# Image 2's routed layer issued in half steps, norms spread a tile earlier: a two-layer attention kernel on one core

## The chip, the core and the metric

The kernel runs on one core of one Trainium2 chip. The metric is the time of one launch on the device in microseconds: 1705.04 us, the median of three runs (1703.87 to 1706.76). The core's engines are called PE or TensorE (matrix products and transposes), DVE or VectorE, ACT or ScalarE, POOL or GpSimd, and SP, which here only issues transfers.

## The reference

The input holds four images of 32 x 128 x 128 floats. Layer 0 turns each image into 128 channels (each 2 x 2 block of pixels gives four) by 64 x 64 places, and lets the channels' rows attend to each other by cosine; here is the core of it:

```python
energy = jnp.einsum('bci,bcj->bij', q, q)
d = jnp.sqrt(jnp.diagonal(energy, axis1=1, axis2=2))
attn = jax.nn.softmax(energy / (d[:, :, None] * d[:, None, :]), axis=-1)
out = gamma * jnp.einsum('bcj,bij->bci', q, attn) + xs
...
t = t + _L1_attn_ref(_ln_t(t), Wk, Wq, Wv)
t = t + _L1_ffn_ref(_ln_t(t), router_w, router_b, expert_w, expert_b)
```

In the kernel's terms: 4096 rows of 128 values per image (after the reshapes), all pairs of rows scored, exponentials, products, a division by the sums. Layer 1 takes the result as tokens of 128 values: a linear attention, which comes down to one 128 x 128 Gram matrix of the normalised tokens per image, a small chain of products of that matrix with the weights, and one product per token; then a router picks two of eight experts for each token and the two expert products are added with their weights.

## The kernel before

**Score tiles.** Each image's 4096 rows are cut into 8 chunks of 512, handled in four pairs kc. `attend` walks over the pairs of chunks jc <= i, four tiles of 128 x 512 for each: 144 tiles per image, 152 for the last image, whose end is ordered differently. A tile is a product `pe` (L607), an exponential on ScalarE with its sum (L610), and a product `po` (L495). Scores are symmetric, so the transposed half is not computed again: VectorE turns 32 x 32 blocks (L419), SP sends them to DRAM and back (L528, L543) to swap them, and some five tiles later TensorE multiplies the turned block (`pg`, L431) while ScalarE sums it (L436).

**The program is an order written by hand.** Everything is a Python generator, and the order of issue on TensorE, VectorE, ScalarE and SP is the order in which the generators are advanced. The loop at the end of the kernel advances `attend` by half a tile: one half ends just before `pe`, the other after the tile's other products. Each other stream that is due is advanced once in each half. So two yields are one tile step of a stream; `idle(n)` is n such steps. GpSimd's operations are pinned to the same order where it matters.

**Streams beside the tiles.** They are of two kinds:

- `timed`: for each image b the preparation of the next one, `prep(b + 1, kc)` for the four pairs of chunks. An entry (steps, begin, end, count) is advanced evenly, count times between begin and end, in per cent of the image. `prep` loads the pixels (L308), turns them into qT, sums squares (L295, L296), takes the power -1/2 on GpSimd (L164), spreads these norms over columns into `wide` (L388, VectorE), transposes `wide` on TensorE into the bank `pnorm` (L397), and multiplies the pixels with it (`scale_all`, L372) to give qn.
- `steady`: layer 1 of an image. It starts at 84% of its own image and runs on through most of the next, one step about every tile. `close_rows(kc)` ends layer 0 for a pair of chunks: transposed sums `pbd`, division (L759), the residual, statistics of each token on VectorE, their power on GpSimd (L164, `rsa`, then `nba` at L688), the normalised rows `xn` on ScalarE (L694), and TensorE's Gram products `pgram` (L726). Then come `matrix` and `attention_rows`, and after them `sorted_experts(h)` for each half h of the tokens.

**Sorted experts.** A half has 2048 tokens with two experts each. VectorE computes where each token goes in a list sorted by expert. GpSimd scatters the rows to DRAM, 32 indirect transfers of 128 rows (L1049). Then the list is read back in 20 pairs of 128-row tiles. For the pair g at position `at` of the loop: SP loads it (L1077) at g, TensorE transposes it (L1118) three positions later, ScalarE copies the transposes out (L1087), TensorE multiplies them with the expert's weights (L1111) at the fourth, VectorE applies the token's weight (L1093) and SP stores the result in `ys` (L1097). A position has two yields: `load` and the evictions of the position before fall into one half of a step, the products into the other.

**Gathers.** After that, GpSimd gathers each token's two results from `ys` and adds them to the token's row in `acc` by indirect transfers that accumulate (L1162): 8 for each group of four tiles, 64 for both halves. `fetch` (on ScalarE's queue, L1147) fills `acc` before, `put` (SP, L1153) writes a finished group to the output. The first half is gathered when the second half's scatters are issued. For images 0 and 1 a gather is issued per step; for image 2 two per step, with a free step after every four (`rate == 2`). Image 3 has no image after it, so it does not sort: `last_parts` multiplies all experts.

**The end.** For image 3 only `close_rows` is a stream (`first_parts`). When the tiles are through, what is left of `steady` is issued, image 2's layer first, then image 3's, and then `last_parts`. The names to follow in the code are `prep`, `close_rows` (`close_stats`, `normalise`, `gram_rows`), `sorted_experts` with `load`, `products`, `fetch`, `put`, and the tuples in the loop at the end.

Of the kernel before, what the change touches and what calls it, by code (L numbers as in the profile page):

```python
# [22 lines left out]
def kernel(  # L23
# [45 lines left out]
    B, C, H, W = x.shape  # L69
# [108 lines left out]
    def idle(n):  # L178
        for _ in range(2 * n):
            yield  # L180
# [167 lines left out]
    def prep(b, kc, st):  # L348

        ahead = 2 if b == 0 and kc == 1 else 5
        xa = load_quarters(b, kc)
        if b == 0:
            load_tokens(st["T"][:, ts(kc, 8), :], b, 8 * kc, 8)
            xx = rows_of_image(b, kc, st)
        for _ in range(ahead):
            yield
        qT = chunks_of(b, kc, st)
        for s in range(2):  # L360
            turn_quarters(s, xa, qT)
            yield
        if b > 0:
            xx = xin.tile([P, 8, HW2, 2], F32, tag="xx", name=f"xx_{b}_{kc}")
            load_tokens(xx.rearrange("p k w r -> p k (w r)"), b, 8 * kc, 8)
        ss = stat.tile([P, 2 * NJ], F32, tag="ss", name=f"ss_{b}_{kc}")

        def scale(s, spread, view):
            qn = channels(b, kc, s, st)
            own = slice(s * 64, s * 64 + 64)  # L370
            for r2 in range(2):
                nc.vector.tensor_tensor(  # L372
                    qn[ts(r2, 64)].rearrange("p (j a t) -> p a j t", a=4, t=S),
                    xx[own].rearrange("p (a k) (h t) r -> p r a (k h) t", a=4, h=2)[:, r2],
                    view(spread[own]),
                    ALU.mult,
                )
        rn = stat.tile([P, 2 * NJ, 1], F32, tag="rn", name=f"rn_{b}_{kc}")
        for s in range(2):
            squares(b, kc, s, qT, ss)  # L380
            if s == 1:
                pow_neg_half(rn[:, :, 0], ss)
            yield
        for _ in range(ahead - 2):
            yield
        wide = work.tile([P, NJ, 2, 64], F32, tag="qs", name=f"wide_{b}_{kc}", bufs=2)
        for s in range(2):
            nc.vector.tensor_copy(wide[:, :, s], rn[:, ts(s, NJ)].to_broadcast([P, NJ, 64]))  # L388
        yield

        def scale_all(bank):
            for s in range(2):
                scale(s, bank, lambda ap: ap.rearrange("p (j a t) -> p a j t", a=4, t=S))

        bank, done = hold(f"pnorm_{b}_{kc}", scale_all)
        for j in range(NJ):
            nc.tensor.transpose(bank[:, ts(j, P)], wide[:, j].rearrange("p s c -> p (s c)"), ident)  # L397
        yield
        done()
        yield  # L400
# [251 lines left out]
    def layer1(b, st):  # L652
# [76 lines left out]
        def close_rows(kc):  # L729


            def missing():
                return len(st["o"]) < 2 * kc + 2 or any(
                    st["got"][c] < NCH - c - (alone and c == NCH - 1) for c in (2 * kc, 2 * kc + 1)
                )

            late_rows = alone and kc >= 2
            last_rows = alone and kc == 3

            while "exps" not in st if last_rows else missing():  # L740
                yield from idle(1)
            while b > 0 and kc == 0 and not states[b - 1].get("sorted"):
                yield from idle(1)
            den, rd = (stat.tile([P, 2 * NJ], F32, tag=nm, name=f"{nm}_{b}_{kc}") for nm in ("den", "rd"))
            nc.vector.tensor_reduce(den, st["sums"][:, ts(kc, 2 * NJ), :], AX.X, ALU.add)
            nc.vector.reciprocal(rd, den)
            wide = work.tile([P, NJ, 2, 64], F32, tag="grp", name=f"rdx_{b}_{kc}", bufs=2)
            for s in range(2):
                one = rd[:, ts(s, NJ)][:, :, None]
                nc.vector.tensor_scalar(wide[:, :, s], one.to_broadcast([P, NJ, 64]), gam, None, ALU.mult)  # L750
            df = work.tile([P, 8, HW2, 2], F32, tag="df", name=f"df_{b}_{kc}", bufs=1)

            def divide(pb):
                for s in range(2):
                    own = slice(s * 64, s * 64 + 64)
                    o = st["o"][2 * kc + s]
                    for r2 in range(2):
                        rows = slice(r2 * 64, r2 * 64 + 64)
                        nc.vector.tensor_tensor(  # L759
                            df[own].rearrange("p (a k) (h t) r -> p r a (k h) t", a=4, h=2)[:, r2],  # L760
                            o[rows].rearrange("p (a j t) -> p a j t", a=4, t=S),
                            pb[own].rearrange("p (j a t) -> p a j t", a=4, t=S),
                            ALU.mult,
                        )

            yield
            if not last_rows:
                yield
                yield
            pb, done = hold(f"pbd_{b}_{kc}", divide)  # L770
            for j in range(NJ):
                nc.tensor.transpose(pb[:, ts(j, P)], wide[:, j].rearrange("p s c -> p (s c)"), ident)
            yield
            while missing():
                yield from idle(1)
            done()
            if not late_rows:
                yield
                yield
            tk = T[:, ts(kc, 8), :]  # L780
            nc.vector.tensor_tensor(tk, tk, df.rearrange("p k w r -> p k (w r)"), ALU.add)
            bs, stats = batch_stats("a", 8 * kc, 8)
            for j in range(8):
                stats[j]()
                if j == 3:
                    yield
                    yield
            close_stats("a", 8 * kc, 8, bs)
            yield from idle(1 if late_rows else 2)
            k = 8 * kc  # L790
            normalise(range(k, k + 4), rsa, nba)
            if late_rows:
                for j in range(k + 4, k + 8):
                    nc.vector.tensor_scalar(
                        xn[:, j, :D], T[:, j, :], rsa[:, j, :], nba[:, j, :], ALU.mult, ALU.add
                    )
            yield
            if last_rows:
                keep_running(36)
                done = gram_rows([k + j // 2 + 4 * (j % 2) for j in range(8)])  # L800
                yield
                done()
                return
            done = gram_rows(range(k, k + 4))
            yield
            done()
            if not late_rows:
                normalise(range(k + 4, k + 8), rsa, nba)
            yield
            done = gram_rows(range(k + 4, k + 8))  # L810
            yield
            done()
            if alone and kc < 3:
                for g in (2 * kc, 2 * kc + 1):
                    yield
                    done = transpose_rows(g)
                    yield
                    done()
# [151 lines left out]
        def sorted_experts(h):  # L970
# [72 lines left out]
            for n in range(2 * HR):  # L1043
# [19 lines left out]
                if n % 4 == 3 and (b < B - 2 or n % 8 == 7):  # L1063
                    yield from idle(1)
            turns[h].append("moved")
            xs_made[h][:], xs_read[h][:] = scatters, []
            yield from idle(3)

# [56 lines left out]
            for at in range(len(pairs) + 5):  # L1125
                if at < len(pairs):
                    load(*pairs[at])
                if done:
                    done()
                yield  # L1130
                turned, applied = (pairs[at - d] if 0 <= at - d < len(pairs) else None for d in (3, 4))
                done = products(turned, applied) if turned or applied else None
                yield
# [22 lines left out]
            rate = 1 if b < B - 2 else 2  # L1156
            fetch(groups[0])
            yield from idle(2)
            for g in groups:
                for n in range(8):  # L1160
# [5 lines left out]
                    if (n + 1) % rate == 0:  # L1166
                        yield
                        yield
                    if rate == 2 and n % 4 == 3:
                        yield from idle(1)  # L1170
                    if n == 3 and g != groups[0]:
                        put(g - 1)
                    if n == 3 and g != groups[-1]:
# [197 lines left out]
    timed = [(first, 0, 1, 2), (second, 0.5, 5.5, 10)]  # L1371
    for b in range(B):
# [5 lines left out]
            timed.append((setup_sorting(), 58, 98, 17))  # L1378
        if b + 1 < B:
            nxt = states[b + 1]  # L1380
            timed.append((prep(b + 1, 0, nxt), 52, 78, 16))
            timed.append((prep(b + 1, 1, nxt), 80, 99, 16))
        if b > 0:
            timed.append((input_rows(b, states[b]), 36, 47, 9))
        done = [0] * len(timed)
# [21 lines left out]
                pass  # L1407
        timed = []
        if b + 1 < B:
            timed.append((prep(b + 1, 2, nxt), 1, 22, 16))  # L1410
            timed.append((prep(b + 1, 3, nxt), 28, 52, 16))
    for steps, _ in steady:
        for _ in steps:
            pass
# [40 lines left out]
```

## Time and profile before

| | |
|---|---|
| median of three runs | 1705.04 us |
| the profiled execution | 1704.18 us |
| its span, first to last instruction | 1702.4 us |
| mean granted TensorE clock | 0.987 |
| score tiles of image 0, 1, 2, 3 begin at | 12.9, 355.9, 749.5, 1148.1 us |
| last exponential of image 3 | 1562.0 us |
| scatters of image 2 | 1299.3 to 1409.1 us |
| gathers of image 2 | 1449.8 to 1603.0 us |

The busiest engines and the costliest groups of the page:

```profile
PE 1629.5 (96%) x5288; PEld 858.7 (50%) x5288; DVE 910.2 (53%) x2343; ACT 913.3 (54%) x2863; POOL 630.5 (37%) x565
...
L1162 POOL DMA_INDIRECT acc<-ys,place x192 | 301.4, 1570 | 300.1 <-ACT pr L610 171.2
...
L726 PE MATMUL pgram<-xn 128*128 128x128 f32 x256 | 38.7, 294 | 34.7 <-ACT xn L694 34.4
```

A group's line gives the source line, engine, operation and tiles, then the busy time in all and the mean of one in ns, then the idle time of the engine just before these instructions and what ended most of it. "xn L694" stands for the instruction on ScalarE whose end released the waiting one. The time of the launch is some 2 us more than the span, which begins with the first instruction and ends with the last.

### The profile page before, as it was taken

To read this page: it belongs to the slowest core of one execution; us is meant where nothing else is said; L and a number is where in the kernel's file an instruction comes from. 1 tells how busy PE (TensorE), PEld (TensorE's weight loads), DVE (VectorE), ACT (ScalarE), POOL (GpSimd) and SP (SyncE) were. 2 spreads that over 40 slices of the span, in tenths; PEclk is the share of its full clock that TensorE was granted. 3 is DMA by queue.
4 is the path that set the end of the run, shared out by engine and by line. 5 is a ranking of instruction groups with operands and counts; after the bars stand their busy time and mean duration, and the time that the engine had idled before them with its cause. 6 is when DMAs were issued, how large, how long until landed. Compare 5 with 4: busy or idle time off the path is not lost.

```text
span 1702.4 us, 21468 instructions
## 1 busy us (share of the span) xinstructions
PE 1629.5 (96%) x5288; PEld 858.7 (50%) x5288; DVE 910.2 (53%) x2343; ACT 913.3 (54%) x2863; POOL 630.5 (37%) x565
## 2 busy tenths in 40 slices
PE   8999999999999999999999999999998999999288
PEld 5444444455544455555554455555554455546243
DVE  5443353666684443567486343557479333346187
ACT  3555445465655555556574555546565455555076
POOL 1000000001034532455454541454555540567666
PEclk9999999999999999999999999999999999999699
DMA  5554765654457777975688777895777867983201
GB/s 159 180 203 145 216 207 198 236 187 156 158 180 254 234 241 220 253 223 163 191 237 243 242 223 226 248 257 155 198 213 223 264 220 224 249 239 59 44 12 39
DMA packets 249067, 332.81 MB, mean 195 GB/s; under 512 B 31984, under 2 KB 176496, under 8 KB 234608
## 3 DMA queue, kind: packets, MB, share of 16 engines
q1 hardware_dynamic: 207312, 291.92, 53.5%
q0 software_dynamic: 33792, 25.58, 8.5%
q10 hardware_dynamic: 7840, 13.93, 2.7%
q8 instruction: 45, 0.74, 0.2%
q14 instruction: 78, 0.64, 0.1%
HBM read 160.78 MB, written 175.80 MB: 198 GB/s over the span
## 4 chain that ended last, share of the span: by engine, by line
PE 77%; DVE 10%; DMA 4%; POOL 3%; ACT 2%; issue 2%; SPq 1%; DVEq 0%; ACTq 0%; POOLq 0%
PE po L495 22%; PE pe L607 21%; PE pg L431 19%; PE pys L1111 3%; PE py L1247 2%; POOL acc L1162 2%; PE pgram L726 2%; PE pg L451 2%; DVE F L419 2%; PE pys L1118 1%; PE pat L852 1%; DVE df L759 1%; DMA blocks<-F 1%; SPq L543 1%; DMA F<-blocks 1%
## 5 line engine op out<-in xcount | busy, mean ns | idle before, releaser
L610 ACT ACTIVATE pr<-pe 128x512 f32<-128x512 f32 (+1 forms) x576 | 322.4, 560 | 533.1 <-PE pe L607 427.7
L495 PE MATMUL po<-pr,qT 128*128 128x512 f32 (+3 forms) x1152 | 551.2, 560 | 3.5 <-ACT o L500 2.2
L607 PE MATMUL pe<-qn,qn 128*128 128x512 f32 x896 | 459.1, 594 | 5.2 <-ACT pr L610 5.0
L431 PE MATMUL pg<-F,qT 128*128 128x512 f32 x880 | 450.3, 593 | 1.6 <-DMA F<-blocks 1.6
L1162 POOL DMA_INDIRECT acc<-ys,place x192 | 301.4, 1570 | 300.1 <-ACT pr L610 171.2
L419 DVE STREAM_TRANSPOSE F<-pr 128x512 f32<-128x512 f32 x440 | 307.4, 703 | 157.1 <-ACT pr L610 124.4
L495 PEld LDWEIGHTS po<-pr,qT 128*128 128x128 f32 x1152 | 215.0, 190 | 250.4 <-issue 223.6
L436 ACT ACTIVATE junk<-F 128x512 bf16<-128x512 f32 x440 | 272.7, 620 | 1.7 <-DMA F<-blocks 1.7
L431 PEld LDWEIGHTS pg<-F,qT 128*128 128x128 f32 x880 | 167.2, 191 | 197.0 <-issue 179.8
L1049 POOL DMA_INDIRECT xs<-xn,place x192 | 185.0, 963 | 165.5 <-ACT pr L610 99.8
L607 PEld LDWEIGHTS pe<-qn,qn 128*128 128x128 f32 x896 | 154.3, 190 | 116.2 <-issue 103.0
L440 DVE TENSOR_TENSOR o<-o,pg 128x512 f32<-128x512 f32 x110 | 75.2, 684 | 207.6 <-PE pg L431 185.7
L164 POOL TENSOR_TENSOR rn<-ss,neg_half 128x8 f32<-128x8 f32 (+1 forms) x17 | 27.7, 1629 | 388.7 <-DVE ss L296 388.7
L1093 DVE TENSOR_TENSOR results<-pys,xn 128x256 f32<-128x256 f32 x120 | 49.8, 415 | 183.8 <-ACT xn L1087 146.3
L610 ACT ACTIVATION_READ_ACCUMULATOR pr<-pe 128x1 f32 x576 | 111.8, 194 | 0.0
L1087 ACT ACTIVATE xn<-pys 128x256 f32<-128x256 f32 x120 | 45.3, 378 | 114.1 <-PE pys L1118 98.1
L1111 PEld LDWEIGHTS pys<-ew_sb,xn 128*128 128x128 f32 x468 | 70.2, 191 | 50.4 <-issue 48.8
L607 PE MATMUL pe<-qn 128*128 128x512 f32 (+3 forms) x256 | 91.0, 438 | 0.7 <-ACT qn L342 0.7
L436 ACT ACTIVATION_READ_ACCUMULATOR junk<-F 128x1 f32 x440 | 84.2, 191 | 0.0
L694 ACT ACTIVATE xn<-T,nba,rsa 128x128 f32<-128x128 f32 x120 | 49.2, 483 | 44.6 <-POOL nba L688 44.6
L726 PE MATMUL pgram<-xn 128*128 128x128 f32 x256 | 38.7, 294 | 34.7 <-ACT xn L694 34.4
L1111 PE MATMUL pys<-ew_sb,xn 128*128 x468 | 71.6, 274 | 0.0
(214 smaller groups left out, 1459.8 us busy)
## 6 DMA issues: line engine op xcount, KB each, us to landing
blocks<-F SPq DMA_DIRECT2D x110, 1024.0 KB
F<-blocks SPq DMA_DIRECT2D x220, 192.0 KB
F<-blocks SPq DMA_DIRECT2D x220, 128.0 KB
xn<-xs SPq DMA_DIRECT2D x114, 132.0 KB
ys<-results SPq DMA_DIRECT2D x114, 128.0 KB
F<-blocks SPq DMA_DIRECT2D x220, 64.0 KB
below<-F SPq DMA_DIRECT2D x31, 384.0 KB
T<-in_x_dram SPq DMA_DIRECT2D x64, 128.0 KB
```

The costliest lines, as they stand in the source:

```text
L419: f()
L431: nc.tensor.matmul(pg.rearrange("p (a f) -> p a f", a=4), st["qT"][i][:, ib, :], G[:, :, ib], start=(ib == 0), stop=(ib == NJ - 1),)
L436: nc.scalar.activation(junk, G[:, :, ib], AF.Copy, accum_out=st["sums"][:, NJ * i + ib, jc : jc + 1])
L440: nc.vector.tensor_tensor(st["o"][jc], st["o"][jc], pg, ALU.add)
L495: nc.tensor.matmul(row["po"][:, lo:hi], qT[blk // NJ][:, blk % NJ, :], w, start=start, stop=(row["left"] == 0))
L607: nc.tensor.matmul(pe[:, c0:], qn[jc][:, ts(j, P)], qn[i][:, c0:], start=True, stop=True)
L610: nc.scalar.activation(pr[:, c0:], pe[:, c0:], AF.Exp, accum_out=sums[:, t, i : i + 1]).ins
L726: nc.tensor.matmul(p[:, :D], xn[:, k, :D], xn[:, k, :D], start=(k == rows[0]), stop=(k == rows[-1]))
L1049: inst = nc.gpsimd.indirect_dma_start(xs[h], offset(place[:, i, k : k + 1]), xn[:, k, :], None)
L1093: nc.vector.tensor_tensor(result[:, :n], p[:, 2 * P : 2 * P + n * D].rearrange("p (j c) -> p j c", c=D), bufs[g % 6][:, :n, D : D + 1].to_ ...
L1111: nc.tensor.matmul(p[:, 2 * P + j * D : 2 * P + j * D + D], bufs[6 + g % 2][:, j, :D], weights[:, bass.ds(begins[2 * (g % 2) + j], D)], st ...
L1162: inst = nc.gpsimd.indirect_dma_start(accs[g][:, n % 4, :], None, ys, offset(place[:, i, k : k + 1]), compute_op=ALU.add)
```

## The change

Six edits, all in the order of issue; no operation is added or removed and nothing of the arithmetic differs.

1. `prep`: for images after the first, one more yield between the spreading of the norms (`wide`) and the transposes that read it.
2. `close_rows`: three idle steps instead of two between the statistics and the first normalised rows (all but the last two pairs of chunks of image 3, which keep one).
3. `sorted_experts`, image 2 alone (`hurried`): the yield between the evictions and the products of a position goes, so that a position takes half a step.
4. The free step after every four gathers of image 2 goes.
5. The counts of `prep` for images 1 to 3 are 17 instead of 16.
6. The third pair of chunks is prepared between 0.5% and 16% of the image instead of between 1% and 22%.

```diff
@@ prep
         for s in range(2):
             nc.vector.tensor_copy(wide[:, :, s], rn[:, ts(s, NJ)].to_broadcast([P, NJ, 64]))
         yield
+        if b:
+            yield
@@ close_rows
             close_stats("a", 8 * kc, 8, bs)
-            yield from idle(1 if late_rows else 2)
+            yield from idle(1 if late_rows else 3)
@@ sorted_experts
             turns[h].append("moved")
+            hurried = b == B - 2
...
                 if done:
                     done()
-                yield
+                if not hurried:
+                    yield
                 turned, applied = (pairs[at - d] if 0 <= at - d < len(pairs) else None for d in (3, 4))
                 done = products(turned, applied) if turned or applied else None
                 yield
...
                     if (n + 1) % rate == 0:
                         yield
                         yield
-                    if rate == 2 and n % 4 == 3:
-                        yield from idle(1)
@@ the loop at the end
-            timed.append((prep(b + 1, 0, nxt), 52, 78, 16))
-            timed.append((prep(b + 1, 1, nxt), 80, 99, 16))
+            timed.append((prep(b + 1, 0, nxt), 52, 78, 17))
+            timed.append((prep(b + 1, 1, nxt), 80, 99, 17))
...
-            timed.append((prep(b + 1, 2, nxt), 1, 22, 16))
-            timed.append((prep(b + 1, 3, nxt), 28, 52, 16))
+            timed.append((prep(b + 1, 2, nxt), 0.5, 16, 17))
+            timed.append((prep(b + 1, 3, nxt), 28, 52, 17))
```

## The prediction

> **What bounds the kernel now.** I read the page's 40 slices first, then the busy times by stretch, then who waited for whom around the hole, then GpSimd's timeline there.
>
> ```profile
> PE   8999999999999999999999999999998999999288
> POOL 1000000001034532455454541454555540567666
> PEclk9999999999999999999999999999999999999699
> ```
>
> TensorE is full nearly everywhere: what is added to its queue costs its own length, and what another engine does is free. The exception is slice 38, where it is 20% busy and its clock falls.
>
> ```profile
> 1449.00:1562.00 113.00, 113.00 (x385) 60.66 (x384) 50.34 (x120) 61.13 (x191) 71.92 (x48) 1.00 0.75 194
> 1562.00:1605.00 43.00, 12.98 (x94) 10.65 (x92) 10.54 (x38) 6.17 (x15) 36.44 (x25) 0.71 0.36 58
> ```
>
> The columns are TensorE, its weight loads, VectorE, ScalarE, GpSimd, then clock, DMA share and GB/s. While image 3 attends, TensorE has no hole at all; from 1562 to 1605 only GpSimd works (36.4 of 43 us).
>
> ```profile
> ACT xn L694 <- POOL nba L688: 34.1, 2, 33.3
> PE pgram L726 <- ACT xn L694: 29.6, 1, 29.6
> ```
>
> TensorE waits 29.6 us for ScalarE's normalised rows, and ScalarE 33.3 us for a scale from GpSimd.
>
> ```profile
> 1599.62 1.54 POOL L1162 DMA_INDIRECT acc<-ys,place  x1 [0.31 <-issue]
> 1601.46 1.54 POOL L1162 DMA_INDIRECT acc<-ys,place  x1 [0.30 <-issue]
> 1602.45 2.27 POOL L164 TENSOR_TENSOR rsa<-dm_a,neg_half 128x8 f32<-128x8 f32 x1
> ```
>
> That scale (the last pair of chunks of image 3) stands in GpSimd's queue behind the last gathers of image 2, one every 1.84 us (1.54 and 0.30 of issue). VectorE had finished its input at 1575.1 (the last sv_a of its timeline); the rows began at 1605.0. So the last layer of image 2 is late, not image 3.
>
> Two smaller holes come back with each image:
>
> ```profile
> PE pnorm L397 <- DVE F L419: 5.8, 3, 2.0
> ```
>
> and two waits of 2.1 us at L726 on ScalarE (tile 14 of images 2 and 3, in the timeline). After two of the three pnorm waits the clock is at half for 3.4 us (508.6 and 907.9).
>
> **What the Trainium skill says.** "DMA: Bandwidth & Descriptors", section "SWDGE vs HWDGE vs iDMA": a transfer that accumulates can be issued by GpSimd alone, whose cores compute the descriptors. The trace agrees: GpSimd is busy 1.54 us per gather of 128 rows, whether DMA is busy (1464) or quiet (1590). So the gathers have a floor of 64 x 1.84 = 118 us. "Trainium Architecture — The Big Picture", section "Inside one NeuronCore": each engine has its own instruction stream and meets the others through semaphores. So a small operation behind a gather waits for the gather, as at 1602. "TensorE: Matmul & The Clock Gate", section "What's actually happening": an idle window of about 3.4 us halves the clock until a busy one. Here the clock was at 0.5 from 1580.3 to 1611.1, and 16 Gram matmuls took 3.79 us where 8 took 0.89.
>
> **The change part by part.** A "tile" is one of the 144 score tiles of an image (152 in image 3), about 2.58 us of TensorE. I counted tiles at which each piece is issued in both programs, and took the tiles' times from the trace before.
>
> 1. *Half steps.* Image 2's pairs of sorted tiles (20 in each half) are issued twice per tile step instead of once. The first half's loop ends at tile 93, not 105; the second's at 116, not 128. The work is moved, not changed: a pair costs 0.66 us of TensorE (steps with a pair take 3.24, without 2.58). But in the old loop the transposes of a pair, the copy L1087 on ScalarE and the product that reads it were a whole step apart. Now every second product follows directly upon the transposes of the pair before it: nothing stands between the end of one step and the start of the next. TensorE then waits for ScalarE. From the timeline at 1398: TensorE is free at 1398.54, the copy starts 0.20 later, takes 0.38, then a handover of about 0.1 and a weight load of 0.11 to 0.19: 0.8 us. The programs show 16 such joints, 8 in each half: 13 us added. This wait is not in the trace; bounds are 0.5 (16 x 0.5 = 8) and 1.5 (24), should loads be late too. It can't gain. The loads L1077 are issued in SP's order behind stores that wait for VectorE; they land in 1.5 to 4.5 us by the DMA packets, and some 4 half steps (8 us) lie between, so I take no wait for them.
>
> 2. *Gathers.* With the first half's products done earlier, and without the free steps, the first gather moves from tile 109 to 102, the last four from the end of the program to tiles 137 and 138. Tile 102 began at 1426.8; 4 more pairs (2.6) and 8 joints (6.4) lie before it: 1436, against 1449.8 before. But 8 gathers need 14.7 us, and 4 tiles without pairs only 10.3. GpSimd keeps pace until group 4 (tile 122, now about 1503: 1486.5, 6 pairs, 13 us of joints), then lags. The 64 gathers end near 1565, while VectorE's input for the last scale comes at 1575 plus all delays. So the hole closes: 1605.0 less 1577.7 (1575.1, the power 1.7, the bias, handovers) is 27.4 us, and 2.7 us more as the clock stays up (16 Gram matmuls 3.79 to 1.78, six at L837 0.7). Gain 30.
>
> 3. *What is late next.* The first scale of image 3 (chunks 0 and 1) is issued at tile 136, behind 60 gathers. From 1504: groups 4 to 6 and four of group 7 are 28 x 1.84 = 51.5, so the power starts at 1555.6 and rows can start 2.2 later (1529.38 to 1531.56 before): 1557.8. ScalarE reaches them after the score of tile 139, a tile later than before because of idle(3): 1533.1 + 1.2 + 13 = 1547. It stands 10.7 us, with all the exponentials of later tiles behind it in its queue. TensorE needs the rows 1.4 us later than they used to be ready (1534.61 against 1533.2), so it stands 9.3 us, and about 2 more at half clock. Bounds: 0, if GpSimd keeps pace, and 17, if gathers take 2.1 us each. SP's stores of finished groups (L1153) also wait for gathers: that of group 5, about 1535, stands before the loads of the last turned block; these land near 1544 and are used at 1553. Hidden, with 9 us to spare.
>
> 4. *Norms, idle(3), third pair of chunks.* The copies to `wide` move ahead of the transposes by a tile, in all three images, and the third pair's to tile 9 from 14. The pnorm waits (5.8) go, with two half-speed windows (2 x 1.7). The Gram waits at tile 14 (2 x 2.1) go, as VectorE's squares for the next image no longer stand before the statistics, and the rows are asked for later. Sum 13.5. Against it, rows of four groups now fall on tiles 4 to 7 in a row, where ScalarE has 0.75 + 0.81 + 1.64 = 3.2 us per tile against TensorE's 3.0, and everything of the last layer is issued a tile later. I take 10 (bounds 4 and 14).
>
> Sum: -30 + 13 + 9.3 + 2 - 10 = -15.7. The profiled execution took 1704.18 us (its span is 1702.4): 1688.5. The median of the runs is 0.86 above it: 1689.
>
> **The rivals.**
>
> *A, GpSimd keeps pace.* If gathers find enough room, the scale at tile 136 isn't waited for: 11 us less, 1678. For it: part 3 rests on a count of 28 gathers without a gap. Against it: bursts in the trace never go below 1.84.
>
> *B, the half steps starve TensorE: slower.* The place is L1111/L1118 of image 2, tiles 81 to 116. If the loads or SP's order make each of the 40 pairs wait, not only the joints, the loss grows. For it: SP stood up to 8 us at L543 with loads behind. Against it: DMA share is 0.70 there, and the step gets longer as pairs get denser. At 2 us for each of 16 joints (32 us, 19 more than forecast) the time is 1708. It decides from 1.8 us per joint.
>
> *C, the hole stays in part.* If the gathers lag further (2.3 us each in the crowded stretch) the last scale is again behind them and the first wait doubles: part 3 costs 25 and the time is about 1702, no change.
>
> *D, joints cheap and small holes wholly gone:* 8 instead of 13, 13.5 instead of 10: 1680, within the forecast's own range.
>
> **How the numbers follow.** Forecast (with D) 0.60, A 0.17, B 0.15, C 0.08. The likeliest case's own range is 1680 to 1698. To leave out no more than two in ten the range takes in A to 1674 and the near part of B and C: 1673 to 1706. Two runs of this kernel tell about 0.2% apart (3.4 us). Faster: forecast and A, 0.77, and a little of C: 0.79. Same: most of C: 0.06. Slower: B: 0.15.
>
> **What would show it.** The hole after 1562 should shrink from 29.6 us to under 3, with GpSimd's last gather before the last rsa. L726 should wait for L694 about 9 us near the first rows of image 3. The pys products should wait 16 times for L1087, about 0.8 us each. pnorm should no longer wait for VectorE. The forecast is wrong if pys waits exceed 25 us in sum, or if SP's stores hold back the turned blocks so that L431 waits for DMA.

## The result and the profile after

| | before | after |
|---|---|---|
| median of 12 runs each | 1704.40 us | 1709.78 us |
| lowest and highest | 1701.27, 1707.55 | 1707.21, 1711.81 |
| span of the profiled execution | 1702.4 us | 1707.7 us |
| mean granted clock | 0.987 | 0.989 |

The ratio is 1.0029, with a 95% interval of 1.0020 to 1.0037: the change made the kernel slower by 0.3%. 1689 us had been forecast.

The hole at the end did close. The slices of the page after, to be held against the same three rows before:

```profile
PE   8999999999999999999999999999999989897888
POOL 1000000010024532455464541545455534577166
PEclk9999999999999999999999999999999999998999
```

The 2 and the 6 of slice 38 are gone. Instead TensorE has an 8 at slices 33 (1366 to 1409 us) and 35, and a 7 at 37 (1537 to 1580). Two stretches by engine (columns: TensorE, its weight loads, VectorE, ScalarE, GpSimd, clock, DMA share, GB/s):

```profile
1360.00:1525.00 165.00, 149.39 (x520) 77.79 (x519) 52.83 (x104) 72.23 (x230) 83.00 (x66) 1.00 0.78 218
...
1562.00:1605.00 43.00, 34.37 (x138) 21.36 (x139) 22.41 (x65) 21.11 (x63) 15.94 (x13) 0.88 0.15 25
```

From 1562 to 1605 TensorE is busy for 34.4 us where it was busy for 13.0. But in the stretch of image 2's sorted products it now stands for 15.6 us, where it had stood not at all. Who makes TensorE wait (sum, times, longest):

```profile
PE pgram L728 <- ACT xn L696: 11.6, 2, 11.1
PE pe L609 <- ACT pr L612: 11.2, 3, 3.8
PE pys L1114 <- ACT xn L1090: 7.9, 14, 1.3
...
PE pys L1121 <- DMA xn<-xs: 4.1, 3, 2.2
PE pys L1114 <- issue: 2.6, 5, 0.5
```

The waits of 29.6 us at the Gram matmuls and of 5.8 at pnorm have gone. In their place stand one of 11.1 at the Gram matmuls, three of 3.7 to 3.8 at the scores, and some twenty small ones at the products (L1114) with a few for loads (L1121).

To divide the loss among the steps, take the exponentials of the score tiles (L612, 144 per image and 152 in image 3) as mileposts and subtract their start times before from those after. Where that shift grows, time is lost:

| stretch | forecast | shift grows by |
|---|---|---|
| start of image 0 to start of image 1 | 0 | +2.2 |
| image 1 to tile 80 of image 3 | -10 | -5.9 |
| tiles 80 to 128 of image 3: sorted products | +13 | +24.8 |
| tiles 139 to 140: first rows of image 3 | +11.3 | +13.0 |
| behind the last tile: the hole | -30 | -28.1 |
| all, with -0.8 in the tiles between | -15.7 | +5.3 |

Where a gain or a loss was forecast, its sign is right. But the third line is 12 us off, the second 4, the fourth and the fifth some 2 each, and the first was not forecast at all.

**The joints.** A joint is a place where a product follows directly upon the transposes of the pair before it. TensorE at a joint of the kernel after, tile 89 (start, duration, instruction; in brackets the idle time before it):

```profile
1394.39 1.02 PE L433 MATMUL pg<-F,qT 128*128 128x512 f32 x2
1395.35 0.71 PE L1114 MATMUL pys<-ew_sb,xn 128*128 x4
1395.90 0.38 PE L1121 MATMUL pys<-ident,xn 128*128 128x128 f32 x2
1396.83 0.70 PE L1114 MATMUL pys<-ew_sb,xn 128*128 x4 [0.55 <-ACT xn L1090]
```

and ScalarE at the same moment:

```profile
1394.93 0.37 ACT L1090 ACTIVATE xn<-pys 128x256 f32<-128x256 f32 x1
1396.38 0.39 ACT L1090 ACTIVATE xn<-pys 128x256 f32<-128x256 f32 x1 [1.08 <-PE pys L1121]
```

The transposes of a pair start at 1395.90, their copy at 1396.38, and the product that reads the copy at 1396.83: 0.93 us in series, with nothing else in TensorE's queue. The first product of the step is not free either. Its copy stood behind the score's sum on ScalarE and ended at 1395.30; the product started 0.05 later. The wait of 0.55 in brackets is only about half of what the step lost: steps with two pairs last 4.91 us, and 2.58 + 2 x 0.66 is 3.90.

SP's order adds to this. At tile 109 a store of a finished group holds SP for 3.9 us, the load behind it is issued late, and TensorE waits for its rows:

```profile
1464.01 3.91 SPq L1157 DMA_DIRECT2D out_dram<-acc  x4
1468.02 0.39 SPq L1080 DMA_DIRECT2D xn<-xs  x1
...
1472.02 0.44 PE L1121 MATMUL pys<-ident,xn 128*128 128x128 f32 x2 [1.62 <-DMA xn<-xs]
```

**The first rows of image 3.** Where the shift jumps by 13 us:

```profile
1565.10 1.54 POOL L1166 DMA_INDIRECT acc<-ys,place  x1 [0.30 <-issue]
1566.08 2.27 POOL L164 TENSOR_TENSOR rsa<-dm_a,neg_half 128x8 f32<-128x8 f32 x1
...
1568.67 0.88 ACT L696 ACTIVATE xn<-T,nba,rsa 128x128 f32<-128x128 f32 x2 [13.49 <-POOL nba L690]
...
1569.21 0.58 PE L728 MATMUL pgram<-xn 128*128 128x128 f32 x1 [11.07 <-ACT xn L696]
```

Gathers fill GpSimd up to the scale of chunks 0 and 1 (L164). ScalarE stands 13.5 us for that scale, and TensorE 11.1 for ScalarE. This is the old hole's wait again, 36 us earlier and about a third as long.

**Tile 52 of images 1 to 3.** ScalarE in image 3:

```profile
1290.36 0.31 ACT L890 ACTIVATE prob<-prob 128x128 f32<-128x128 f32 x1 [4.31 <-DVE prob L889]
```

It stands 4.3 us at the router's exponential, with the next score's exponential behind it. What VectorE did meanwhile:

```profile
1285.23 0.65 DVE L295 TENSOR_TENSOR sq<-qT 128x512 f32<-128x512 f32 x1
...
1286.52 0.68 DVE L295 TENSOR_TENSOR sq<-qT 128x512 f32<-128x512 f32 x1
1287.24 0.69 DVE L296 TENSOR_REDUCE ss<-sq 128x4 f32<-128x512 f32 x1
...
1290.03 0.29 DVE L889 TENSOR_TENSOR prob<-lg,weight 128x128 f32<-128x128 f32 x1
```

Both squares of the fourth pair of chunks now stand ahead of the router. (They are this image's own: the first two pairs of chunks are prepared while the image before attends, the last two while their own image does.) Before, the second one came after it and ScalarE waited 1.6 us:

```profile
1289.64 0.31 ACT L888 ACTIVATE prob<-prob 128x128 f32<-128x128 f32 x1 [1.60 <-DVE prob L887]
...
1290.15 0.65 DVE L295 TENSOR_TENSOR sq<-qT 128x512 f32<-128x512 f32 x1
```

From tile 50 to 56 of image 3 the shift grows by 5.7 us, though the wait is 3.7: a stretch of 3.4 us at half clock follows (from 1292.5 us) and takes 1.7. The shift in so short a stretch also holds work of layer 1 that idle(3) issues a tile later, so it isn't all loss.

### The profile page after: what moved, and what is told of

Same layout as the page of the kernel before. It is cut to its first block, busy times and chain, and to the rows that moved or that the text cites. A ratio compares the mean times of both kernels' runs of the same rounds, so it can differ in the third digit from the quotient of the medians.

```text
span 1707.7 us, 21473 instructions
## 1 busy us (share of the span) xinstructions
PE 1638.6 (96%) x5288; PEld 857.7 (50%) x5288; DVE 907.0 (53%) x2343; ACT 910.4 (53%) x2863; POOL 629.6 (37%) x565
## 4 chain that ended last, share of the span: by engine, by line
PE 78%; DVE 7%; DMA 6%; ACT 3%; SPq 2%; issue 2%; POOL 2%; ACTq 0%; DVEq 0%; POOLq 0%
PE po L497 23%; PE pe L609 22%; PE pg L433 19%; PE pys L1114 3%; PE py L1249 3%; DMA blocks<-F 2%; PE pg L453 2%; PE pgram L728 2%; PE pys L1121 1%; PE pat L854 1%; SPq L545 1%; DMA F<-blocks 1%; POOL acc L1166 1%; DVE F L421 1%; DMA acc<-t 1%
## 5 line engine op out<-in xcount | busy, mean ns | idle before, releaser
L612 ACT ACTIVATE pr<-pe 128x512 f32<-128x512 f32 (+1 forms) x576 | 322.6, 560 | 586.5 <-PE pe L609 509.5
L164 POOL TENSOR_TENSOR rn<-ss,neg_half 128x8 f32<-128x8 f32 (+1 forms) x17 | 27.2, 1601 | 336.2 <-DVE ss L296 322.0
L612 ACT ACTIVATION_READ_ACCUMULATOR pr<-pe 128x1 f32 x576 | 111.9, 194 | 0.0
L1114 PEld LDWEIGHTS pys<-ew_sb,xn 128*128 128x128 f32 x468 | 67.5, 191 | 67.6 <-issue 37.8
L1114 PE MATMUL pys<-ew_sb,xn 128*128 x468 | 75.5, 283 | 11.8 <-ACT xn L1090 7.9
L164 POOL TENSOR_TENSOR rsa<-dm_a,neg_half 128x8 f32<-128x8 f32 x16 | 27.9, 1744 | 118.2 <-DVE sv_a L688 118.2
L1249 PE MATMUL py<-ew_sb,xn 128*128 128x512 f32 x128 | 61.3, 621 | 5.4 <-ACT tmp L1206 4.2
```

The costliest lines, as they stand in the source:

```text
L164: pinned(nc.gpsimd.tensor_tensor(dst, src, neg_half.to_broadcast(list(src.shape)), ALU.pow))
L612: nc.scalar.activation(pr[:, c0:], pe[:, c0:], AF.Exp, accum_out=sums[:, t, i : i + 1]).ins
L1114: nc.tensor.matmul(p[:, 2 * P + j * D : 2 * P + j * D + D], bufs[6 + g % 2][:, j, :D], weights[:, bass.ds(begins[2 * (g % 2) + j], D)], st ...
L1249: nc.tensor.matmul(bank, xn[:, k, :D], ew_sb[:, 4 * h : 4 * h + 4, :], start=True, stop=True)
```

## The experiments

Each kernel was timed in turn with the kernel before on the same chip. The ratio is to the kernel before, with its 95% interval. A difference between two experiments is one of their medians; where the two were not timed together, the ratios give up to 2 us more or less. "The shift" is that of the score tiles against the kernel before, as in the table above.

**full_steps** takes the half steps out of the changed kernel and keeps all else.

```diff
-                if not hurried:
-                    yield
+                yield
```

> The changed kernel with image 2's sorted pairs again in whole steps; gathers without free steps, norms and third pair as changed. Theory J (the half steps themselves cost about 24.6 us between tiles 81 and 128, and 12.9 at the first rows of image 3 because the gathers come in a burst): both go, the hole stays closed, since only 4 gathers are issued behind the last score tile against 20 before. Span about 1707.7 - 24.6 - 11 = 1672, so 1674 timed, about 1.8% faster than before. Rival G (the denser gathers crowd the DMA queues and SP, the half steps are harmless): the loss between tiles 81 and 128 stays in large part, 1695 or more.

1686.08 us, ratio 0.9888 (0.9874 to 0.9902). Between tiles 80 and 128 TensorE has no idle time at all and the shift against before stays within 0.7 us, so rival G falls: gathers back to back every 1.84 us cost TensorE nothing. The span is 1686.5; the 14.5 us that it lies above 1672 are at the end. GpSimd there:

```profile
1563.65 1.55 POOL L1164 DMA_INDIRECT acc<-ys,place  x1 [0.30 <-issue]
1564.63 2.28 POOL L164 TENSOR_TENSOR rsa<-dm_a,neg_half 128x8 f32<-128x8 f32 x1
...
1573.42 1.55 POOL L1164 DMA_INDIRECT acc<-ys,place  x1 [0.30 <-issue]
1574.41 2.26 POOL L164 TENSOR_TENSOR rsa<-dm_a,neg_half 128x8 f32<-128x8 f32 x1
```

The scales of chunks 2 and 3 and of chunks 4 and 5 each stand behind the gathers issued before them, and TensorE waits 5.07 and 7.69 us. "4 gathers left" was the wrong thing to count: what matters is how far GpSimd lags when each scale is issued.

**half_alone** adds the half steps alone to the kernel before (the yield goes for image 2; gathers keep their free steps).

> The kernel before with half steps alone: gathers keep their free steps, norms and third pair as before. Theory J: tiles 81 to 128 lose about 24; the gathers begin 8 tiles sooner, 8 instead of 20 are left behind the last score tile, so the hole loses 22 to 29 us, and the first rows of image 3 are not waited for long (the gathers are paced): span 1702.4 + 24 - 26 = 1700, no change within 0.4%. Rival G (the denser gathers made the loss): tiles 81 to 128 lose 13 at most, 1688.

1706.01 us, ratio 1.0008 (1.0000 to 1.0017). Between tiles 80 and 128 its shift grows by 20.7 us, with 20 waits of TensorE at L1111, 15 of them put down to the copy, and none for a load:

```profile
PE pys L1111 <- ACT xn L1087: 9.7, 15, 1.3
```

So a joint costs 20.7 / 20 = 1.03 us on average, with the gathers still paced. The first rows of image 3 aren't waited for here, and the gain at the end pays for the joints without anything left over.

**no_joints** keeps the half steps but lets each product come one position later, so that a copy and its product are no longer neighbours.

```diff
-            for at in range(len(pairs) + 5):
+            for at in range(len(pairs) + 5 + hurried):
+                if done and hurried:
+                    done()
                 if at < len(pairs):
                     load(*pairs[at])
-                if done:
+                if done and not hurried:
                     done()
...
-                turned, applied = (... for d in (3, 4))
+                turned, applied = (... for d in (3, 4 + hurried))
```

> The changed kernel with each product of image 2 one half step later, so that a pair's copy on ScalarE and the product that reads it are never neighbours; one more half step in each half. Theory J1 (the loss of 24.6 us is half joints, half loads behind SP's waits): about 12 to 15 us less, 1693 to 1697 timed. J2 (all joints): 1685. Rival L (loads late, SP held; joints are nothing): 1705 to 1710.

1698.21 us, ratio 0.9968 (0.9955 to 0.9981): 11.6 us less than the changed kernel, a little short of J1. A two-pair step of TensorE now:

```profile
1395.35 1.02 PE L433 MATMUL pg<-F,qT 128*128 128x512 f32 x2
1396.20 0.61 PE L1114 MATMUL pys<-ew_sb,xn 128*128 x4
1396.65 0.38 PE L1121 MATMUL pys<-ident,xn 128*128 128x128 f32 x2
1396.87 0.61 PE L1114 MATMUL pys<-ew_sb,xn 128*128 x4
```

Without the copy between them the undisturbed steps last 3.90 us, not 4.91. That settles the price of a joint, and the starts say where it goes: from the transposes to the next product it is 0.22 us here and 0.93 at the joint (0.71 more), and the other three steps, from `pg` to the first product and from each product to its transposes, are 0.1 shorter each. But the waits change their name:

```profile
PE pys L1121 <- DMA xn<-xs: 9.1, 7, 3.4
```

By the code, the extra position takes a half step from the loads' lead, since a buffer of rows comes free one position later. Of the 24.8 us, 13.7 are still lost between tiles 80 and 128.

**act_loads** is no_joints with image 2's loads issued by ScalarE (`nc.scalar` for `nc.sync` at L1080).

> no_joints with image 2's loads of sorted pairs issued by ScalarE instead of SP. Theory S (loads are late because SP stands in a store or a block load that waits for a transfer, with the loads behind it): the product's waits for loads fall from 9.1 us to under 3, 1690 to 1692. Rival D (DMA is full there, share about 1.0, and loads land late whoever issues them): they stay at 7 or more, 1696 to 1700. If issuing on ScalarE costs it more than it saves, the waits turn up at L609 on ScalarE and the time is above 1700.

1695.39 us, ratio 0.9943 (0.9927 to 0.9959), 2.8 us less than no_joints. The waits for loads fall from 9.1 to 1.7, so the loads were late because of SP's order, not because the DMA queues were full. Little was gained, since ScalarE now stands itself:

```profile
1453.20 0.46 ACTq L1080 DMA_DIRECT2D xn<-xs  x1
1453.70 0.60 ACT L612 ACTIVATE pr<-pe 128x512 f32<-128x512 f32 x1 [5.08 <-DVE results L1096]
```

A load waits in ScalarE's queue until VectorE has left its buffer, and a score's exponential waits behind it. Theory S was right on the loads, and its time was missed by 3 us for this reason.

**later_puts** is the changed kernel with image 2's stores of finished groups four gathers later (n == 7 in place of n == 3 for `put(g - 1)`).

> The changed kernel with image 2's stores of finished groups issued four gathers later, so that SP doesn't meet group 0's store (3.9 us on SP at 1464) just ahead of a load of sorted pairs. Theory S (late loads are SP's order): the wait of 1.62 us for a load at tile 109 goes, the one of 2.18 at tile 105 (behind six block loads) stays; 1 to 3 us less between tiles 104 and 116, which the timing may not tell from nothing: 1707 to 1710. Rival D (full DMA queues): both waits stay.

1706.10 us, ratio 1.0005 (0.9994 to 1.0016). That is 3.7 us less than the changed kernel, more than was expected. The load wait at tile 109 is gone and that tile lasts 4.38 us, not 6.22, as theory S has it. The one at tile 105 stays (1.87); a half-clock window followed it in this profile (0.50 from 1447 to 1450), and tiles 105 and 106 lasted 2.4 us longer, so that tiles 80 to 128 show no gain (25.4 for 24.8). In the profiles the difference lies elsewhere: 2.8 us at the first rows of image 3 and 2.4 between image 1 and tile 80 of image 3, where no half-clock stretch followed the wait at tile 52 of image 2. So the store's order is shown to make the one late load, but not to be worth 3.7 us. That the late load at tile 105 comes from the block loads ahead of it rests on SP's timeline alone; no run isolates it. In the changed kernel the two late loads cost 1.8 us at tile 109 and 2.4 at tile 105 (7.31 us for an undisturbed 4.91).

**after_paced2** is the changed kernel with the free steps back for the second half's gathers.

```diff
+                    if rate == 2 and h == 1 and n % 4 == 3:
+                        yield from idle(1)
```

> The changed kernel with the free step after every four gathers put back in the second half of image 2 alone. Theory W (the wait of 11.1 us at the first rows of image 3, 12.9 us of time, comes from the burst of gathers before the scale of chunks 0 and 1, as the prediction's part 3 has it): 50 instead of 60 gathers stand before that scale, so the wait falls to 0 to 4 us; at the end two gathers' groups still end before the last score tile: 9 to 13 us less than 1709.8, so 1697 to 1701. Rival: the wait comes from VectorE's statistics: it stays, 1709.

1697.71 us, ratio 0.9967 (0.9954 to 0.9979), 12.1 us less than the changed kernel. The wait of 11.1 us at L728 is gone (TensorE waits nowhere near these rows for 1 us or more), and no hole opens at the end. 52 gathers now stand before the scale, not 60. The burst of gathers made the wait; nothing of it was VectorE's.

**prep_alone** is the kernel before with edits 1, 2, 5 and 6: norms, idle(3), counts and third pair.

> The kernel before with the norm's copies a tile ahead, the third pair sooner, 17 steps and idle(3) alone; pairs in whole steps, gathers with free steps. The trace after shows 5.9 us gained up to tile 80 of image 3, and the hole at the end is untouched (20 gathers behind the last score tile): span 1702.4 - 6 - 1 = 1695 to 1697, 0.35% faster. If the prediction's term of 10 was right and something else took 4 of it: 1692.

1699.80 us, ratio 0.9969 (0.9957 to 0.9980), a gain of 5.3 us (3.4 to 7.3) where 0.35% was expected. The three waits of 3.7 us at tile 52 are all here, so they belong to these edits.

**gathers_alone** is the kernel before with edit 4 alone, the free steps gone.

> The kernel before with the gathers' free steps left out, and nothing else. full_steps against prep_alone gives this part 13.8 us (0.9888 against 0.9969). If the parts add up: 1704.5 - 13.8 = 1691 (1688 to 1694), with two waits of 5 and 7.7 us left at the end in the place of one of 29.6. If the part needs the others' help: 1697 or more.

1691.43 us, ratio 0.9939 (0.9920 to 0.9958). The parts add up: 0.61% here and 0.31% for prep_alone make 0.92%, and the two together (full_steps) give 1.12% (0.98 to 1.26). This one edit closes most of the hole: TensorE finds waits of 4.4, 1.2 and 5.1 us where there was one of 29.6.

**full_c16** is full_steps with the fourth pair's count at 16 again, which puts the two squares at tiles 50 and 51.

```diff
-            timed.append((prep(b + 1, 3, nxt), 28, 52, 17))
+            timed.append((prep(b + 1, 3, nxt), 28, 52, 16))
```

> full_steps with the fourth pair of chunks spread over 16 steps again instead of 17, so that the two squares on VectorE are issued at tiles 50 and 51 and not both at 50; the layer-1 stream stays a tile later. Theory Q (the new waits of 3.7 us at tile 52 of images 1 to 3 come from both squares standing before the router's exponential on VectorE): these three waits fall under 1 us each, and with them the half-clock windows behind them; between tiles 50 and 56 of image 3 the changed kernel loses 5.7 us, so 3 x 3.7 to 3 x 5.7 = 11 to 17 us less than 1686: 1669 to 1675. Rival R (the later start of the layer-1 stream, idle(3), makes them): they stay at 3.7, and the time is 1686.

1677.88 us, ratio 0.9829 (0.9807 to 0.9851): 8.2 us less than full_steps, which falls short of Q's 11 to 17. The waits shrink, but stay:

```profile
PE pe L609 <- ACT pr L612: 7.1, 3, 2.4
```

From tile 50 to 56 of image 3 the shift grows by 4.3 where it grew by 6.5. So the squares explain 1.35 us of each wait, and rival R had a share. Up to tile 80 of image 3 this one count is worth 9.2 us: the shift falls by 14.4 us from the start of image 1, and by 5.1 in full_steps. About 3.4 of the 9.2 is half clock, of which full_steps had 13.6 us behind these waits and this profile 6.8.

**mixed_idle2** (below: best_mixed with idle(2) for idle(3)) asked for that share.

> best_mixed with idle(2) in place of idle(3) behind the statistics, so that the layer-1 stream stands a tile earlier again, as in the kernel before. Theory R (what was left of the wait at tile 52 in full_c16, 2.36 us in each of images 1 to 3, comes from the router falling a tile later): the waits fall under 0.7 us, and 6 to 12 us go with the half-clock windows, 1661 to 1667, unless the first rows of each image are then waited for again at tile 14 (2 x 2.1 in the kernel before), which would leave 1665 to 1670. Rival: the wait stays at 2.4, 1672.

1680.39 us, ratio 0.9859 (0.9843 to 0.9875). The waits at tile 52 are gone: from tile 50 to 56 the shift doesn't grow at all. So what had stayed was the layer-1 stream's later tile, R. No wait of 2.1 us returns at tile 14 either, so there the third pair's earlier place (edit 6) is enough without idle(3).

Yet the time is 7.6 us above best_mixed. Up to tile 80 of an image TensorE waits as long as there (3.3, 3.3 and 4.4 us in images 1 to 3, against 3.6, 3.2 and 3.2), since other waits came: 0.6 and 0.5 at tiles 49 and 51, as in the kernel before, and 0.9 to 1.0 at tile 57:

```profile
PE pcnt L1001 <- DVE runs L992: 2.8, 3, 1.0
```

By the shifts of the two profiles, 1.9 of the 7.6 us were lost before image 1, 4.6 between there and tile 80 of image 3, 2.2 in tiles 80 to 128, and some 2 at the first rows of image 3, which are asked for a tile sooner and wait for GpSimd (4.63 us at tile 139, against 2.10); the end is 3.5 us better, in spite of a wait of 7.49 behind the last tile. What the 4.6 us are made of stays open.

**best** is full_c16 with the first fetch of each half issued inside the loop over the pairs and no idle steps behind it, so that the gathers start four tiles sooner.

```diff
+            sooner = b == B - 2
             for at in range(len(pairs) + 5):
+                if sooner and at == len(pairs) + 2:
+                    fetch(groups[0])
...
-            yield from idle(1)
+            if not sooner:
+                yield from idle(1)
...
-            fetch(groups[0])
-            yield from idle(2)
+            if not sooner:
+                fetch(groups[0])
+                yield from idle(2)
```

> full_c16 with the first fetch of each half of image 2 issued before the loop's end and no idle steps behind the loop: the gathers start 4 tiles sooner (tile 107), the last two are issued at tile 148. In full_steps two waits are left at the end, 5.07 us for chunks 2 and 3 behind 56 gathers, and 7.69 for chunks 4 and 5 behind 60. Theory F (GpSimd's floor of 1.84 us per gather from the first gather on sets both): 62 gathers now stand before chunks 2 and 3, which end at about 1441 + 114 + 7 = 1562, so the first wait stays, and the second goes: 7 to 8 us less than full_c16, 1662 to 1668. Rival: the waits come from VectorE's own chain (15.35 us of wait at L796 notwithstanding): no gain over full_c16.

1680.58 us, ratio 0.9849 (0.9831 to 0.9866): no better than full_c16. The wait of 7.67 did shrink, to 3.9, and that of 5.07 to 3.2. But 46 gathers, not 40, now stand ahead of the scale of chunks 0 and 1, and TensorE waits 9.26 us for it at tile 140. The expectation had counted chunks 2 to 5 and forgotten the first ones.

**best_mixed** is best with the free steps kept in the second half, as in after_paced2.

> best with the free step after every four gathers kept in the second half of image 2 (4 gathers in 3 tiles, 7.4 us of GpSimd in 7.7): 8 gathers are left behind the last score tile. Theory F: chunks 0 to 3 of image 3 are not waited for, chunks 4 and 5 for about 5 us at most: 3 us less to 3 us more than best. If the floor isn't what decides, both times agree within 1 us with full_c16.

1672.81 us, ratio 0.9809 (0.9790 to 0.9828): the fastest of all, 1.9% under the kernel before, and so about 2.2% under the changed one. Chunks 0 to 5 are waited for 2.1 to 2.3 us at most. That is 7.8 us under best, more than the 3 expected, because best's loss at tile 140 hadn't been foreseen. It is also 5.1 under full_c16, but there the intervals overlap. One wait is left, 6.43 us for the scale of the last chunks behind the last eight gathers:

```profile
1570.26 1.54 POOL L1169 DMA_INDIRECT acc<-ys,place  x1 [0.30 <-issue]
1571.26 2.26 POOL L164 TENSOR_TENSOR rsa<-dm_a,neg_half 128x8 f32<-128x8 f32 x1
```

VectorE had finished that scale's input at 1566.4.

## Why the prediction was wrong

**Part 1, the half steps, is the step that failed.** The mechanism was right: the product follows its own transposes and waits for the copy on ScalarE. It was mis-sized twice, and a cost was put at nothing. The prediction had 16 joints at 0.8 us, 13 us; half_alone shows 20 at 1.03 with no other wait mixed in, 20.7 us. The count missed the joint at the start of each loop (tiles 81 and 104) and the second one in the tiles of a diagonal block (84 and 112). The price of 0.8 was near for the product that it was worked out for (0.71). But it left out 0.3 us in the rest of the step: the first product starts on the heels of its copy too, since the copy stands behind the score's sum on ScalarE (1394.93 above), and both groups of products take 0.1 longer up to the transposes behind them. Then "I take no wait for them": two loads came late, at tiles 105 and 109, behind block loads and a store in SP's order, for 4.1 us more. 20.7 + 4.1 is the 24.8 of the table. The trace before had a sign of this, which the prediction itself names under rival B: SP stood for 8 us at L543 with loads behind, as long as the whole lead of 8 us that the loads were given.

Rival B had the outcome, slower, but not the cause. It had loads or SP's order make the pairs wait, and put 2 us on each of 16 joints; of the 24.8 us only 4.1 are late loads, and B's turning point (1.8 x 16 = 29 us in part 1) wasn't reached. Other terms did the rest: of the 21 us between -15.7 and +5.3, part 1 made 11.8, part 4 4.1, the start 2.2, part 3 1.7 and the hole 1.9, with -0.8 in the tiles between.

**Part 2, the gathers and the hole**, held: the hole gave -28.1 (-30). The first gather at 1436.5 (1436 forecast) is luck in part: the tiles before it came 3.7 us sooner, which this sum had left out, and its ten joints took some 4 us more than the eight that it counted. gathers_alone shows that the hole needed only edit 4.

**Part 3, the first rows of image 3**, held: 13.0 us for 11.3, and the scale began at 1566.1, 10.5 later than reckoned, as part 1 had held up products and gathers alike. after_paced2 shows the burst as the cause.

**Part 4, norms, idle(3) and third pair**, had the right sign and too large a size: 5.9 in the traces, 5.3 in prep_alone, for 10. The waits at pnorm and at tile 14 went as forecast. What failed is that nothing was put down for edit 5, nor for the tile on which idle(3) puts the router: the new wait of 3.7 us at tile 52, three times, was not foreseen. Two of the edits make it together: idle(3) moves the router onto a tile where 2.4 us are waited for it (full_c16; none in mixed_idle2), and the count of 17 puts both squares ahead of the router, 1.35 us more. What the count of 17 does with idle(2) was not run. The 10 us were to be had: with the fourth pair's count at 16 the same stretch gains 14.4 (full_c16), and 10.7 with idle(2) as well (mixed_idle2).

**The start.** 2.2 us were lost before image 1 begins. They were lost before tile 30 of image 0 (2.8 there), in code that no edit touches: the first edited lines come at about half of that image. After 12 us the clock was at 0.72 on average to 18 us, and again from 22 to 28; in the profile of before it was 1.00 in both. half_alone, whose image 0 is also unchanged, shows the same two windows and 3.1 us, gathers_alone neither. So this is no effect of the change, and in a single pair of profiles it is nearly half the difference between the two kernels.

The range (1673 to 1706) ended below the result because nearly everything missed in one direction. Part 1 at 24.8, a little above its upper bound of 24, would have made 1701 with all else as forecast, still inside; the other terms added 9. Of these the start is bad luck.

## What to carry to other kernels

When a pipeline over several engines is issued twice as densely, price the chain that had been a whole step apart: transposes, copy, product. Count every neighbouring pair in the generated order of each engine, not in the loop's regular part, and take the price from start to start, not from the idle time in brackets.

Look first for the smallest edit that reorders the queue which makes a hole. Here one removed idle step in the gathers was worth 0.6%, and the half steps that were to help it cost more than they brought.

When work moves earlier on an in-order queue, list everything small that stands behind it at each later time, first rows included; pacing the long jobs to just under the queue's rate (four gathers of 1.84 us in three tiles of 2.58) was worth 12 us in one kernel (after_paced2) and 8 in another (best_mixed).

A wait that is removed can come back elsewhere. idle(2) took away three waits of 2.4 us at tile 52, and TensorE waited nearly as long in sum at tiles 49, 51 and 57: add up an engine's waits over the whole stretch before calling one of them a gain.

## What the runs showed of the hardware

TensorE lost nothing to dense gathers: in full_steps tiles 80 to 128 of image 3 ran without a recorded gap, though from 1451 us on GpSimd issued a gather every 1.84 us and the DMA share, by stretches of 10 us, was 0.9 to 1.1 up to 1510. The contention that rival G feared did not appear.

What a wait on TensorE costs depends on what the clock does after it. The wait at tile 52 stands alone in its stretch, so that images with and without a half-clock stretch behind it can be compared:

| kernel, image | wait, us | half clock in tiles 50 to 56, us | shift grows by, us |
|---|---|---|---|
| full_c16, image 2 | 2.35 | 0 | 2.6 |
| full_c16, images 1 and 3 | 2.38, 2.36 | 3.4 | 4.3 |
| later_puts, image 2 | 3.71 | 0 | 4.0 |
| later_puts, image 3 | 3.71 | 3.4 | 5.7 |
| later_puts, image 1 | 3.81 | 6.8 | 6.7 |

One half-clock stretch of 3.4 us adds 1.7, half its length. Whether it comes is not settled by the wait's length: equal waits in the same kernel have it and don't. The Trainium skill, "TensorE: Matmul & The Clock Gate", section "What's actually happening", has the monitor's window of about 3.4 us running free, without regard to a kernel's start. The runs agree: with the same code of image 0, half-clock stretches before 28 us are there in some profiles and absent in others, for -0.1 to +3.2 us at tile 30.
